# A gated cross-attention and feed-forward kernel: the first feed-forward layer by two levels of seven products, over blocks of 1024 tokens

## The chip, the cores and the metric

The kernel runs on one core of a Trainium2 chip. The core has five engines with a queue of instructions each: TensorE (PE in the profile, with its weight loads as PEld), VectorE (DVE), ScalarE (ACT), GpSimd (POOL) and SyncE (SP), which here issues nearly all DMAs. TensorE multiplies a stationary 128x128 tile (lhsT) by a moving tile and writes to PSUM, which has eight banks of 512 float32 per partition; the other engines work on SBUF, and ACT and DVE on PSUM too. The metric is the device time of one execution in microseconds (us), the median over runs. All data is float32.

## What is computed

Four sequences of 2048 tokens of width 512 attend to 128 context tokens each, and then pass a feed-forward network (FFN) with one of eight experts, chosen once per sequence. Cut to what matters:

```
x = x + tanh(g_xattn) * xattn(layernorm(x), ctx)
z = layernorm(x)                                   # (4, 2048, 512)
top1 = argmax(mean(z, tokens) @ Wr + br)           # one expert for each sequence
h = relu(z @ W1[top1] + b1[top1])                  # 512 -> 2048
out = x + tanh(g_ffn) * (h @ W2[top1] + b2[top1])  # 2048 -> 512
```

## The kernel before

**Stages.** For the first sequence ("batch" 0) attention and normalization of its four blocks of 512 tokens run ahead of everything else, with pools of their own (line 226 on). After that the FFN of batch b runs block by block, and the attention of batch b+1 is woven in: `attention` and `route` are generators, and the loop from line 671 advances them by one step at some of the `yield`s of `ffn`. Attention leaves x (after attention) and the normalized z, transposed, in DRAM tiles (`x1d`, `z2d`); `route` picks the expert, reads its number into a register (line 361) and loads its biases. The order in which instructions are emitted gives their priority; a scheduler places them on the engines' queues and adds the semaphores.

**The two FFN layers.** Each layer's matrix product is split into 2x2 quarters on each side and done with seven products of quarters in place of eight (the form with 15 sums). `chain` (line 447) issues the matmuls of one product into one bank. The sums of the operands are made beforehand: of z on DVE (`z_combine`, line 475), of the weights on POOL (`w1_combine`, `w2_combine`), of h on DVE (lines 557, 558, 617, 618). The seven results are put together by ACT copies (lines 529, 592) and DVE additions that read PSUM (lines 533 to 554, 607 to 642). Where two products belong to the same output, the second goes on accumulating in the bank of the first (`fresh` is False).

The first layer (lines 499 to 561) runs over a block of 512 tokens and four groups of hidden columns: each of the seven products of a group takes 2 x 2 matmuls with 256 moving columns, 112 matmuls for a block. W1 is loaded anew for each block and group (`w1_load`, 256 KB pieces in a pool of 13 buffers), and its sums are made anew on POOL. Line 522 applies bias and relu on ACT. The second layer (lines 589 to 647) has seven products of 16 matmuls each, 112 for a block; W2 is loaded once for each batch and its sums are made once. Line 584 adds each result, scaled, to the residual `xr`, which POOL has given the bias (line 564), and two stores per block write the output.

**PSUM.** After the first phase there are five banks for the FFN (`ps_f`), two for transposes and one for attention.

## Time and profile before

| | us |
|---|---|
| median of 3 runs | 1820.86 (1819.43 to 1821.22) |
| profiled execution | 1823.6 |
| its span, first to last instruction | 1821.8 |
| mean granted TensorE clock, share of full speed | 0.988 |

| stretch, us | PE busy | DVE busy | ACT busy | POOL busy | granted clock | GB/s |
|---|---|---|---|---|---|---|
| 0 to 50 | 37.10 | 26.64 | 5.45 | 4.68 | 0.97 | 282 |
| 50 to 100 | 46.50 | 28.30 | 29.37 | 4.22 | 0.93 | 171 |
| 100 to 150 | 37.77 | 15.54 | 7.01 | 28.18 | 0.86 | 273 |
| 150 to 200 | 36.93 | 22.94 | 14.84 | 25.63 | 0.83 | 106 |
| 300 to 600 | 300.00 | 134.49 | 62.59 | 103.13 | 1.00 | 116 |
| 1671.07 to 1767.90, one FFN block alone | 96.83 | 36.96 | 16.81 | 20.26 | 1.00 | 54 |

The span begins with the first instruction and ends with the last; the run's own time lies a little above it. A busy time counts an engine from the start of an instruction to its end; for PE matmuls are pipelined, so that a busy PE need not be at its peak. The granted clock is the share of TensorE's full clock that the throttle let through. In the groups of instructions a line has the source line, the engine, the operation, output and input by name, shapes and count, then the busy time, the mean of one in ns, and the engine's idle time just before with what ended it.

### The profile page before, as it was taken

How to read it: one execution, taken by the hardware profiler on the slowest of the kernel's cores; microseconds unless marked ns; L12 is line 12 of the kernel's file. 1: busy time of each engine (PE TensorE's matmuls, PEld its weight loads, DVE VectorE, ACT ScalarE, POOL GpSimd, SP SyncE). 2: the span in 40 equal slices, each digit the busy share in tenths (PEclk: the TensorE clock that was granted, in tenths of full speed). 3: DMA queues.
4: the chain of work that ended last, by engine and by line, in shares of the span. 5: the costliest groups of instructions: out<-in, count | busy, mean ns of one | idle time of the engine just before them, and what ended most of it. 6: DMA issues, size and time to landing. Idle time of an engine off the chain costs nothing.

```text
span 1821.8 us, 21727 instructions
## 1 busy us (share of the span) xinstructions
PE 1766.8 (97%) x8336; PEld 1515.9 (83%) x8336; DVE 829.1 (46%) x1283; ACT 393.1 (22%) x941; POOL 555.6 (30%) x376
## 2 busy tenths in 40 slices
PE   7977999999999999999999999999999999999998
PEld 5546788888888888788888888788888888888887
DVE  4615446454434645464353545555344434444342
ACT  1422213121111313223030322313021111212030
POOL 0137215032325504124051813204043632314030
PEclk9988999999999999999999999999999999999999
DMA  7373334241243425343132434314133322212100
GB/s 288 157 297 110 130 149 152 85 159 52 93 139 108 147 87 168 116 156 117 65 98 106 137 129 162 129 68 145 36 116 116 116 70 92 71 71 92 69 24 24
DMA packets 62167, 211.45 MB, mean 116 GB/s; under 512 B 8048, under 2 KB 8048, under 8 KB 47344
## 3 DMA queue, kind: packets, MB, share of 16 engines
q1 hardware_dynamic: 60336, 208.20, 32.7%
q10 hardware_dynamic: 1728, 1.86, 0.3%
q8 instruction: 66, 1.08, 0.2%
q14 instruction: 37, 0.30, 0.0%
HBM read 158.13 MB, written 51.90 MB: 115 GB/s over the span
## 4 chain that ended last, share of the span: by engine, by line
PE 89%; DVE 3%; POOL 3%; DMA 2%; issue 2%; ACT 1%; SPq 0%; ACTq 0%; POOLq 0%; DVEq 0%
PE Z L451 24%; PE V L451 23%; PE X L451 22%; PE Y L451 12%; PE psc L161 3%; PE pav L191 2%; PE pt L214 1%; PE pv L292 1%; DVE st L146 1%; DVE x L192 1%; DMA w<-in_W_dram 1%; POOL w2t L444 1%; DMA bqk_t<-in_bqk_dram 1%; PE pk L266 1%; POOL w2t L441 0%
## 5 line engine op out<-in xcount | busy, mean ns | idle before, releaser
L522 ACT ACTIVATE h<-c,b1T 128x256 f32<-128x256 f32 x384 | 174.0, 500 | 515.3 <-DVE c L541 267.3
L451 PE MATMUL X<-zt,w 128*128 128x256 f32 x1024 | 246.4, 383 | 0.8 <-ACT r L529 0.7
L451 PE MATMUL X<-w,h 128*128 128x256 f32 x1024 | 230.0, 381 | 2.7 <-ACT r L592 2.5
L451 PEld LDWEIGHTS X<-w,h 128*128 128x128 f32 x1024 | 192.6, 190 | 34.6 <-ACT r L592 6.9
L451 PEld LDWEIGHTS X<-zt,w 128*128 128x128 f32 x1024 | 195.3, 192 | 31.0 <-issue 2.9
L406 POOL TENSOR_TENSOR w1t<-w,w1t 128x512 f32<-128x512 f32 x64 | 89.6, 1400 | 370.7 <-issue 368.5
L153 POOL TENSOR_TENSOR rstd<-ve,mhalf 128x4 f32<-128x4 f32 x32 | 33.7, 1052 | 411.5 <-DVE ve L152 360.6
L403 POOL TENSOR_TENSOR w1t<-w,w 128x512 f32<-128x512 f32 x64 | 87.5, 1367 | 200.9 <-PE Z L451 200.4
L529 ACT COPY r<-X 128x512 f32<-128x512 f32 x64 | 36.3, 568 | 441.2 <-PE X L451 441.2
L451 PE MATMUL Y<-s,w1t 128*128 128x256 f32 x512 | 121.7, 380 | 4.3 <-POOL w1t L404 4.3
L451 PE MATMUL Z<-zt,w 128*128 128x256 f32 x512 | 123.2, 383 | 0.0
L451 PE MATMUL V<-s,w1t 128*128 128x256 f32 x512 | 121.5, 379 | 0.0
L451 PE MATMUL Z<-zt,w1t 128*128 128x256 f32 x512 | 121.1, 379 | 0.0
L451 PE MATMUL V<-s,w 128*128 128x256 f32 x512 | 120.9, 379 | 0.0
L557 DVE TENSOR_TENSOR hS<-h,h 128x512 f32<-128x512 f32 x64 | 97.0, 1516 | 49.8 <-ACT h L522 49.7
L451 PE MATMUL Z<-w,h 128*128 128x256 f32 x512 | 117.1, 379 | 0.0
L451 PE MATMUL Z<-w2t,h 128*128 128x256 f32 x512 | 115.8, 379 | 0.0
L451 PE MATMUL V<-w2t,hS 128*128 128x256 f32 x512 | 115.3, 379 | 0.0
L451 PE MATMUL Y<-w2t,hS 128*128 128x256 f32 x512 | 115.1, 379 | 0.0
L451 PE MATMUL V<-w,h 128*128 128x256 f32 x512 | 114.1, 379 | 0.0
L451 PEld LDWEIGHTS Y<-s,w1t 128*128 128x128 f32 x512 | 96.2, 190 | 17.6 <-POOL w1t L404 5.1
L451 PEld LDWEIGHTS Y<-w2t,hS 128*128 128x128 f32 x512 | 97.0, 190 | 16.4 <-issue 3.8
(112 smaller groups left out, 2519.7 us busy)
## 6 DMA issues: line engine op xcount, KB each, us to landing
w<-in_W_dram SPq DMA_DIRECT2D x256, 256.0 KB, 2.7
xT<-in_xT_dram SPq DMA_DIRECT2D x16, 1024.0 KB, 4.9
x<-in_x_dram SPq DMA_DIRECT2D x16, 1024.0 KB, 5.5
x1d<-x SPq DMA_DIRECT2D x16, 1024.0 KB, 3.9
xr<-x1d SPq DMA_DIRECT2D x16, 1024.0 KB, 5.1
z2d<-zT SPq DMA_DIRECT2D x16, 1024.0 KB, 4.5
zt<-z2d SPq DMA_DIRECT2D x16, 1024.0 KB, 4.8
w<-in_W_dram SPq DMA_DIRECT2D x16, 1024.0 KB, 4.9
```

The costliest lines, as they stand in the source:

```text
L146: nc.vector.bn_stats(st, xt[:, t, :])
L153: nc.gpsimd.tensor_tensor(rstd, ve, mhalf, ALU.pow)
L161: nc.tensor.matmul(psc[:, t, :], lhsT=xTt[:, kc, t * P : (t + 1) * P], rhs=Mb[:, kc, :], start=kc == 0, stop=kc == KC - 1,)
L191: nc.tensor.matmul(pav, lhsT=pT[:, t * P : (t + 1) * P], rhs=Vb, start=True, stop=True)
L192: nc.vector.scalar_tensor_tensor(xt[:, t, :], pav, coef[:, t : t + 1], xt[:, t, :], ALU.mult, ALU.add)
L214: nc.tensor.transpose(pt[:, t * P : (t + 1) * P], z[:, t, kc * P : (kc + 1) * P], ident)
L403: eng.tensor_tensor(t1, b12, b11, ALU.subtract)
L406: eng.tensor_tensor(t4, b21, t2, ALU.subtract)
L451: nc.tensor.matmul(bank[:, c, :], lhsT=left(k, c), rhs=right(k, c), start=fresh and c == 0 and k == 0, stop=c == cols - 1 and k == ks - 1, ...
L522: nc.scalar.activation(dst[:, 2 * g + c, :], src[:, c, :], AF.Relu, bias=b1T[:, f : f + 1])
L529: nc.scalar.copy(r1, X)
L557: nc.vector.tensor_tensor(hS[:, sl, :], h["21"][:, sl, :], h["22"][:, sl, :], ALU.add)
```

## The change

The first layer is done by two levels of seven products. The work is cut into stages: a block of 1024 tokens and one half of the hidden columns (`fh`). On the outer level z (1024 x 512) and W1 (512 x 1024) are each cut into quarters and combined to seven operands; each outer product is cut and combined again to seven inner products of 128 x 256 x 256, which take two matmuls each. The second layer keeps one level, on the half of the hidden columns that the stage has, for two halves of the output's token pairs (`cp`); the partial output of the first half of the columns goes to DRAM (`y1d`) and is loaded as the residual of the second.

What goes with it:

- `inner` gives the seven inner products with three banks X, Y and Q. The sums that were made by DVE are now continued in PSUM: ACT copies X to Y and later Y to Q, and further products accumulate on the copy. Six matmuls named "begin" write all six banks once before.
- `ffn1` interleaves the inner products of one outer product with the last three of the one before it. The results of two quadrants are summed by DVE (`done`), those of the other two by DVE and POOL (`summed`), and their activations are put off (`waiting`).
- The weight sums are made once per batch and half by `stage_w1` and `stage_w2` on POOL and stored to DRAM (`W1d`, `W2d`), the stores put off by some steps (`later`, `older`). For the first half of batch 0 `stage_w1_first` makes them on DVE and hands the first tiles on directly. The FFN loads all weights through a ring of eight tiles (`fetch`), 14 for each layer and stage.
- `z_prepare` loads z for 1024 tokens and makes both levels of sums on DVE, during the second layer of the stage before.
- Attention normalizes x in place after its store, which is cut in two; the transposed z shares the pool of x's transpose. `ps_t` has one bank instead of two, `ps_f` six instead of five.
- The weaving is by a clock: each step of the FFN adds 0.87 or 3.46, attention advances one step per 2.2, staging one per 1.45.
- `layouts` arranges W1 and W2 for these loads.

The core of the diff; the two layers' old code (lines 375 to 445 and 465 to 647) is removed:

```diff
     for t in range(4):
...
+            if t % 2:
+                nc.sync.dma_start(x1d[b, blk][:, t - 1 : t + 1, :], xt[:, t - 1 : t + 1, :])
             yield
-        nc.sync.dma_start(x1d[b, blk], xt)
...
-        z = zp.tile([P, 4, H], F32, tag="z", name=f"z_{b}_{blk}")
+        z = xt
...
+    def inner_sums(eng, b, fh, pc, src, lo, n, slot, kinds="AB"):
+        new = stp.tile([P, 3, 4, P], F32, tag="new", name="new", bufs=2)
+        b11, b21, b22, b12 = (src[:, lo : lo + n, i, :] for i in range(4))
+        t3, t2, t4, t1 = (new[:, 0:n, i, :] for i in range(4))
+        for o, l, r in ((t1, b12, b11), (t2, b22, t1), (t4, b21, t2), (t3, b22, b12)):
+            eng.tensor_tensor(o, l, r, ALU.subtract)
+            yield
...
+    def stage_w1(b, fh, eng):
+        for pc in range(2):
+            flush()
+            base = stp.tile([P, 4, 4, P], F32, tag="base", name="base")
+            tt = stp.tile([P, 3, 4, P], F32, tag="tt", name="tt")
+            w1_base(b, fh, pc, base)
+            yield from settle(4)
+            for _ in outer_sums(eng, base, tt):
+                yield from settle(1)
+            for src, lo, n, slot in ((base, 0, 3, 0), (base, 3, 1, 3), (tt, 0, 3, 4)):
+                for _ in inner_sums(eng, b, fh, pc, src, lo, n, slot):
+                    yield from settle(1)
+            yield from settle(AGE + 1)
...
+    def fetch(freed=0):
+        ring["freed"] += freed
+        while ring["issued"] < min(ring["freed"] + NW, len(items)):
+            st, kind, i = items[ring["issued"]]
...
+    def inner(product, copied, summed, done):
+        t = {}
+        def m1():
+            t["X"] = bank("X")
+            product(t["X"], 1, True)
+            t["Y"] = bank("Y")
+            nc.scalar.copy(t["Y"], t["X"])
+        def m7():
+            t["Q"] = bank("Q")
+            product(t["Q"], 7, True)
+            t["s7"] = copied(t["Q"])
+        def m6():
+            product(t["Y"], 6, False)
+            nc.scalar.copy(t["Q"], t["Y"])
+        def m2():
+            product(t["X"], 2, False)
+            done(11, t["X"])
+        def m5():
+            product(t["Y"], 5, False)
+            summed(22, t["s7"], t["Y"])
+        def m4():
+            product(t["Q"], 4, False)
+            summed(21, t["s7"], t["Q"])
+        def m3():
+            product(t["Y"], 3, False)
+            done(12, t["Y"])
...
+        level1(5, 7, 4, ALU.add)
+        yield
+        level1(6, 5, 1, ALU.subtract)
+        level2(5)
+        yield
...
+            def summed(j, a, v):
+                c = first(j) if m == 1 else ctile()
+                nc.vector.tensor_tensor(c, a, v, ALU.add)
+                if m != 1:
+                    sums(m, j, c, nc.gpsimd, c)
+            def done(j, v):
+                if m == 1:
+                    nc.scalar.copy(first(j), v)
+                else:
+                    sums(m, j, v, nc.vector)
...
+        for i in range(8):
+            cur = group(i) if i < 7 else None
+            for k, (who, m) in enumerate((
+                (cur, 1), (last, 5), (cur, 7), (last, 4), (cur, 6), (last, 3), (cur, 2)
+            )):
+                if who:
+                    due = len(waiting) if k in (0, 3) else 0
+                    who[m]()
+                    for _ in range(due):
+                        relu(*waiting.pop(0))
+                    yield
...
+            fetch((cur is not None) + (last is not None))
+            last = cur
...
+            cur[2]()
+            for k in (slice(0, 2), slice(2, 4)):
+                nc.vector.tensor_tensor(
+                    h[12][:, k, cs], h[12][:, k, cs], hS[:, k, cs], ALU.subtract
+                )
+                nc.vector.tensor_tensor(hS[:, k, cs], hS[:, k, cs], h[11][:, k, cs], ALU.add)
+            yield
+            cur[4]()
+            if cp == 0:
+                s2(1)
+            yield
+            cur[5]()
+            store(cp, 1)
+            yield
+            cur[3]()
+            store(cp, 0)
+            yield
...
+    for _ in range(6):
+        bk = bank("begin")
+        nc.tensor.matmul(
+            bk.rearrange("p a q -> p (a q)"), lhsT=ident, rhs=cq, start=True, stop=True
+        )
...
+    run(z_prepare(0, 0))
+    run(route(0))
+    stage_w1_first(nc.vector)
+    bias2_load(0)
+    staged_upto[0] += 1
+    fetch()
+    run(stage_w2(0, 0, nc.gpsimd))
...
+        for blk in range(NF):
+            for fh in range(2):
+                for _ in ffn1(b, blk, fh):
+                    tick(0.87)
...
+                for _ in ffn2(b, blk, fh):
+                    next(prep, None)
+                    tick(3.46)
```

## The prediction

> **What bounds the kernel now.** I read the page's busy shares first, then the chain of work that ended last, then PE's waits, then the groups for durations.
>
> ```profile
> PE 1766.8 (97%) x8336; PEld 1515.9 (83%) x8336; DVE 829.1 (46%) x1283; ACT 393.1 (22%) x941; POOL 555.6 (30%) x376
> ```
>
> TensorE is busy 97% of the span; no other engine reaches half. A busy PE alone proves little, so the chain, in order of time (start, duration, work), around the end of one FFN block:
>
> ```profile
> 1373.54 1.73 PE Z L451 x8
> 1375.26 1.73 PE V L451 x8
> 1376.99 6.91 PE X L451 x32
> 1383.90 0.86 PE Z L451 x4
> 1384.76 7.04 PE X L451 x32
> 1391.80 6.04 PE Z L451 x28
> ```
>
> The chain is matmul after matmul. A float32 matmul shows as two instructions, so a first-layer product (4 matmuls) is 1.73 us and a second-layer one (16) is 6.91 us. The same product returns at 1574.24, 1671.07 and 1767.90: 96.83 us per 512-token block without attention work, 224 matmuls, **0.4323 us each**. After the first 200 us PE waited for 7.6 us in all:
>
> ```profile
> PE Y L451 <- POOL w1t L404: 3.3, 1, 3.3
> PE X L451 <- ACT r L592: 2.5, 2, 1.3
> PE pav L191 <- DVE x L192: 1.8, 2, 0.9
> ```
>
> So time follows the count of matmuls, until something else gets in PE's way. The start is different: the first FFN matmul is at 121.78 us, and over the next 42 us PE is busy 29.84 us at a granted clock of 0.83 (the columns are PE, PEld, DVE, ACT, POOL busy, clock, DMA share, GB/s).
>
> ```profile
> 122.00:132.00 10.00, 8.34 (x29) 6.21 (x30) 0.69 (x1) 0.58 (x1) 9.92 (x6) 0.82 1.04 416
> 122.00:164.00 42.00, 29.84 (x124) 24.93 (x125) 14.56 (x25) 8.06 (x18) 41.76 (x31) 0.83 0.54 206
> ```
>
> The rows from which the rest is priced:
>
> ```profile
> L522 ACT ACTIVATE h<-c,b1T 128x256 f32<-128x256 f32 x384 | 174.0, 500 | 515.3 <-DVE c L541 267.3 <-DVE c L554 151.7 <-DVE c L549 96.0
> L406 POOL TENSOR_TENSOR w1t<-w,w1t 128x512 f32<-128x512 f32 x64 | 89.6, 1400 | 370.7 <-issue 368.5
> L557 DVE TENSOR_TENSOR hS<-h,h 128x512 f32<-128x512 f32 x64 | 97.0, 1516 | 49.8 <-ACT h L522 49.7
> L537 DVE TENSOR_TENSOR u<-u,Z 128x512 f32<-128x512 f32 x64 | 44.0, 688 | 48.3 <-PE Z L451 47.0
> L584 DVE SCALAR_TENSOR_TENSOR xr<-c,gf,xr 128x512 f32<-128x512 f32 x48 | 36.8, 766 | 1.5
> L482 DVE TENSOR_TENSOR zt<-zt 128x512 f32<-128x512 f32 x16 | 11.0, 685 | 0.0
> L617 DVE TENSOR_TENSOR hS<-hS,h 128x1024 f32<-128x1024 f32 x32 | 40.5, 1267 | 53.9 <-PE V L451 53.9
> L529 ACT COPY r<-X 128x512 f32<-128x512 f32 x64 | 36.3, 568 | 441.2 <-PE X L451 441.2
> ```
>
> **Removed: matmuls.** First layer: 49 products of 2 matmuls per stage (1024 tokens, half the hidden columns), 98, against 112 for the same work before. Second layer: 2 x 7 products of 2 x 4 = 112, unchanged. All keep 256 moving columns and the 0.4323 us. A stage is 210 x 0.4323 = 90.8 us (42.4 + 48.4), 16 stages 1452.5 us, against 3584 x 0.4323 = 1549.4 us: **-96.8 us**.
>
> **Added on VectorE.** Per stage: 28 adds with one PSUM operand (0.688) 19.3; 4 + 12 sums of hidden tiles at 0.685 alone, 1.516 beside POOL, 11-24; 12 additions to the output (0.766) 9.2; on alternate stages the bias, 4 x 1.22 = 4.9, or the sums of z, 4 x 1.22 + 28 of 256 elements. No row has 256; between 0.167 (128x8) and 0.685 a line gives 0.42, so 16.6; mean 10.8. Attention of the next batch 13.4 (the rows of lines 146 to 199 over 16 blocks). Together 64 to 77 of 90.8 us, against about 39 of 96.8 before. Worst are the second layers that carry the z sums: 9.2 + 8.2 to 18.2 + 16.6 + 7.1 = 41 to 51 of 48.4 us, six times over three batches. VectorE stays under PE, but runs of several us come before what PE waits for.
>
> The spread stands on line 557: shortest 0.678, median 1.544, and its neighbours without POOL at work 0.685. So about 0.83 us is lost per meeting. The Trainium skill ("SBUF — State Buffer", section "SBUF: two separate sides") goes further against this change: a VectorE operation with two SBUF inputs and a GpSimd operation that reads SBUF exclude each other for a whole instruction, the loser "fully blocks". By that rule each of some 30 such operations per stage could wait a whole 1.40 us instead of 0.83, 17 us more VectorE per stage, and the sum below would move to rival C.
>
> **Added on ScalarE.** Per outer product three copies (X to Y, the seventh product out of PSUM, Y to Q), 1.70 us; 32 activations per stage at 0.45 to 0.50. First layer 12 + 1 + 15 = 28 of 42.4 us, second 3.4, attention 9.0 (lines 175 to 217): 41 of 90.8.
>
> **Added on POOL.** 14 sums x 1.40 = 20 per stage; weight sums 84 per batch (60 of 512 elements' worth). About 47%.
>
> **Added on DMA.** In MiB: weight ring 207 (28 loads of 384 or 512 KB per stage), staging 97, residuals 64, z 16, attention 64, constants 8: 456 MiB, 478 MB against 211.45. At the 416 GB/s of the row above that is 1150 us, under 70% of the span; all goes through SP's queue, some 60 issues of 0.35 us per stage. The exception is the first stage: ring 10, residuals 4, the first W1 and W2 staging 12, the second half's 10, attention 9.5 MiB, 48 MB in 91 us = 530 GB/s, 24 us late, of which the ring of eight tiles (three outer products, about 15 us) covers most.
>
> **What lands on PE's path.** (a) Turns, where a product must continue in a bank that ACT or DVE has just read. In the chain X ends at 1383.90 and resumes at 1384.76: 0.86 us for a 0.58 us copy, so 0.28 of signalling, with two matmuls of Z pulled into the gap. In the first layer two outer products are interleaved: three other products, 2.6 us, lie between a copy and its use, so nothing shows; without that cover each turn costs 0.86. In the second layer product 3 follows 5 in the same bank: 0.766 + 0.28 = 1.05 us, twice a stage. If the next product's matmuls fill it as Z did, about 0.4 stays. With 0.4 for the last outer product, which has no partner, **1.2 us per stage, 15 stages, +18**; bounds 0 and 5 us (1.05 plus one 1.22 us operation ahead of it on VectorE, twice, and 0.4): 0 to +75. Behind a late VectorE, its additions and then product 3 and the ring's releases queue; POOL's sums delay only activations two thirds of an outer product later.
>
> New waits on memory, each costed at 0 with its cover: z overwrites x in place, so ACT waits there for the stores of x1d (2.6 us per 512 KB on the page's DMA list) with the copies of the FFN queued behind it; two paced steps of 2.2 us lie between. The residuals of the second token half are loaded into the buffers of the first, store plus load about 2.6 + 3, first needed 7 us later by VectorE, behind which the hidden sums queue. On SP such a waiting store holds the weight loads behind it; the ring's 15 us cover it. Without these covers each costs PE 2 to 5 us, which is rival C again.
>
> (b) The start. The route is at 114 us as now; then two loads of 1 MiB (some 7 us at 416 GB/s with 2 us of latency, against 256 KB pieces before) and the first sums, so 124 instead of 121.8: **+2** (-5 to +8; the first attention pass gets more buffers, but z now waits for the store of x1d that it overwrites). In the first stage VectorE also makes the weight sums, 56 of 128 elements (0.29 on the same line) and 8 of 512, 22 us, so 41 to 47 + 6 of attention against 42.4 of matmuls, and the DMA is late by up to 9 beyond its cover: **+13** (0 to +30). The old start loses some 12 us over 122 to 164 too, which stays in the base. Six extra matmuls of 512 columns (about 0.86 each, twice the 256-column price) lie in the idle gap before the first weights: 0; without that gap 5.2. The end keeps one addition and one store: 0 (-1 to +2).
>
> **Sum.** 1821.8 - 96.8 + 18 + 2 + 13 = 1758.0 us of span. The profiled execution was 1823.6 with this span, so +1.8, and the median of the runs is 2.7 below that: **1757 us**.
>
> The Trainium skill ("PSUM — Partial Sum Buffer", section "The four PSUM rules") holds that only zero is a safe ScalarE seed for an accumulation and that others go through the PE. No run here shows what a bank does with such a seed. Seeding by a 512-column identity product instead would, by the estimate above, put two more 0.86 us products in each of 112 + 32 sets, 248 us, and undo the change; the code copies instead.
>
> **Rivals.**
> - A, the forecast: 1740 to 1775. Chance 0.50.
> - B, nothing new shows: turns filled, start covered: 1821.8 - 96.8 + 2, less 0.9, about 1726 (1715 to 1740). For it: PE's 7.6 us of waits now. Against: VectorE at 70 to 85% and no spare bank. 0.20.
> - C, a crowded VectorE: meetings with POOL on top, 4 us per stage, in the second layer: 60 instead of 18, 1799 (1780 to 1812). For it: line 557. Against: PSUM-operand adds show 0.688 whatever POOL does. 0.18.
> - D, slower: ACT's copies are late in the first layer. In the last outer products ACT has 1.7 + 3.6 + 1.4 of attention = 6.7 us per 6.05 us of matmuls, in order, and an activation that waits for POOL holds the copy behind it. One exposed turn per outer product, 112 x 0.86 = 96: 1757 + 96 = 1853. It decides from 64 us, 0.57 us per outer product. Against: the 2.6 us of cover. 0.09.
> - E: DMA delivers too little. Slower only below 478 MB in some 1.7 ms, 281 GB/s, against 416 when pressed; 240 GB/s would give about 2 ms. 0.03.
>
> **How the numbers follow.** The point is A's. The range holds A, most of B and C's lower half: 1722 to 1805; A's own range is 1740 to 1775. What this kernel's measurement can tell from no change is about 0.2%, 3.6 us. Faster: A, B and nearly all of C, 0.87; within it C's top, 0.02; slower D and E, 0.11.
>
> **What would show it.** 3360 FFN matmuls, with products of the second layer still 3.46 us per 8; gaps of under 1 us before product 3 of the second layer, released by VectorE's L584-like additions; no PE wait on ScalarE in the first layer (D if there are 112 of them); VectorE near 65% and DMA near 70%; the first FFN matmul near 124 us. I am wrong if PE waits total more than 60 us after 220 us, or if ring loads are what releases matmuls.

## The result, and the profile after

The change made the kernel slower: 1914.41 us (median of 4 runs, 1909.92 to 1921.93) against 1821.04 us (1819.43 to 1824.66) of the kernel before on the same chip, a ratio of 1.0514 (95% interval 1.0475 to 1.0553). 1757 was predicted, 1805 was the top of the range. The profiled execution took 1909.92 us with a span of 1908.1.

The page's busy line of the changed kernel:

```profile
PE 1739.5 (91%) x7900; PEld 1446.0 (76%) x7900; DVE 1039.8 (54%) x1807; ACT 607.4 (32%) x1339; POOL 639.1 (33%) x552
```

The count of TensorE instructions fell by 436: twice the 224 matmuls that were taken away, less twice the six that were added. Only 27.3 us of busy time went with them, though, and the span grew. No engine but TensorE passes 54%; the answer can't be an engine that is full on average. TensorE's waits of the changed kernel from 200 us on (what waited, for whom; us in all, times, longest):

```profile
PE Y L607 <- ACT Q L635: 36.7, 18, 5.8
PE Y L607 <- DVE hS L903: 17.1, 13, 3.6
PE psc L195 <- DVE sc L199: 16.7, 9, 4.7
PE Y L607 <- DVE c L781: 12.8, 14, 1.9
PE Y L607 <- DVE xr L872: 11.4, 7, 3.1
PE Y L607 <- ACT Y L626: 7.0, 3, 3.5
```

Where there were 7.6 us of waits there are now 117 (with five smaller kinds), the largest on ScalarE's copies in the first layer. From 220 us on they sum to 110.7; the prediction had named more than 60 as its sign of being wrong. In the last sequence, which has neither attention nor weight sums beside it, the chain of the changed kernel (start, duration, work) is as before:

```profile
1624.70 0.86 PE Q L607 x4
1625.56 0.86 PE Y L607 x4
1626.43 1.73 PE X L607 x8
1628.15 0.86 PE Y L607 x4
```

Matmul after matmul, at the old price, so the loss lies in particular stages. To find it I added up, from the trace's instruction times, how much longer each interval from one TensorE instruction to the next is than the undisturbed one (0.216 us for 256 columns), and call that the *loss*; it holds waits and slowed matmuls alike. From the first FFN matmul on, the kernel before loses 39.1 us and the changed one 219.1. The sum closes: 1821.8 - 96.8 (matmuls) + 4.1 (first FFN matmul at 125.9 instead of 121.8) - 39.1 + 219.1 = 1909.1, against 1908.1 measured. A loss can shift by 1 to 2 us with the value taken as undisturbed for attention's short matmuls. By the 16 stages, and by first (L1) and second layer (L2):

```
                          what lies beside it            L1 lost   L2 lost
stage 0                   staging and attention             32.6      17.2
stages 2,3,6,7,10,11      staging of the next sequence      60.8      40.3
stages 1,5,9              attention's end, staging's start  37.9      11.9
stages 4,8                attention                          4.0       4.3
stages 12-15              nothing                            4.3       5.8
```

Stages 12 and 14, with nothing beside them, take 93.0 and 92.7 us; the prediction had 90.8 + 1.2. What a loss looks like: the timeline of POOL, those of VectorE and ScalarE (start, duration, operation; in brackets the idle time before and what ended it), then four-microsecond stretches of TensorE alone (PE busy, clock, DMA share, GB/s), all of the changed kernel in stage 10.

```profile
1344.23 1.28 POOL L420 TENSOR_TENSOR tt<-base,tt 128x512 f32<-128x512 f32 x1
1345.46 1.01 POOL L429 TENSOR_TENSOR new<-base,new 128x384 f32<-128x384 f32 x1
1346.41 1.01 POOL L429 TENSOR_TENSOR new<-base 128x384 f32<-128x384 f32 x1
1347.37 1.27 POOL L742 TENSOR_TENSOR u<-r,c 128x512 f32<-128x512 f32 x1
...
1350.38 0.99 POOL L429 TENSOR_TENSOR new<-base,new 128x128 f32<-128x128 f32 x2
1351.32 2.48 POOL L745 TENSOR_TENSOR c<-u,c 128x512 f32<-128x512 f32 x2
```

```profile
1343.86 0.69 DVE L781 TENSOR_TENSOR c<-s,Y 128x512 f32<-128x512 f32 x1 [0.97 <-ACT h L712]
1345.56 0.69 DVE L781 TENSOR_TENSOR c<-s,Q 128x512 f32<-128x512 f32 x1 [1.01 <-PE Q L607]
```

```profile
1344.63 0.59 ACT L772 COPY s<-Q 128x512 f32<-128x512 f32 x1 [0.31 <-PE Q L607]
1352.62 0.91 ACT L712 ACTIVATE h<-c,b1T 128x256 f32<-128x256 f32 x2 [7.41 <-POOL c L745]
1353.43 0.58 ACT L635 COPY Q<-Y 128x512 f32<-128x512 f32 x1
```

```profile
1344.00:1348.00 4.00, 4.00 (x20) 1.00 0.08 27
1348.00:1352.00 4.00, 0.91 (x5) 1.00 0.88 238
1352.00:1356.00 4.00, 1.94 (x5) 0.76 1.05 345
1356.00:1360.00 4.00, 4.00 (x17) 0.81 0.89 261
```

POOL is never idle here, but most of what it does is weight sums (L420, L429); the first layer's sum u (L742) and then c (L745) stand in its queue between them. VectorE had made the operands of the two sums of L745 by 1344.55 and 1346.25; the first of them starts at 1351.32. ScalarE sits for 7.41 us in front of the activation that waits for that c, with the copy Y to Q behind it, and TensorE, which needs the copied bank, loses 5.3 us there. The clock falls as well: the stretches after the gap show 0.76 and 0.81 in the mean, and the trace's clock record has 0.50 from 1354.07 to 1357.48.

The start of the changed kernel, with the columns of the prediction, to be set against the line of 122 to 164 us before:

```profile
126.00:168.00 42.00, 32.83 (x136) 24.84 (x135) 37.34 (x103) 16.30 (x42) 11.11 (x9) 0.91 0.70 229
```

VectorE's 37.34 of 42 us are weight sums, adds and attention, where the prediction had 41 to 47 plus 6 for the first layer of this stage.

### The profile page after: what moved, and what is told of

The parts are those of the page before. It is cut to its first block, busy times and chain, and to the rows that moved or that the text cites. A ratio compares the mean times of both kernels' runs of the same rounds, so it can differ in the third digit from the quotient of the medians.

```text
span 1908.1 us, 22980 instructions
## 1 busy us (share of the span) xinstructions
PE 1739.5 (91%) x7900; PEld 1446.0 (76%) x7900; DVE 1039.8 (54%) x1807; ACT 607.4 (32%) x1339; POOL 639.1 (33%) x552
## 2 busy tenths in 40 slices
DMA packets 186659, 479.86 MB, mean 251 GB/s; under 512 B 17328, under 2 KB 71088, under 8 KB 175920
## 5 line engine op out<-in xcount | busy, mean ns | idle before, releaser
L607 PE MATMUL Y<-z,w 128*128 128x256 f32 x1344 | 352.3, 395 | 61.7 <-ACT Q L635 38.3
L607 PEld LDWEIGHTS Y<-z,w 128*128 128x128 f32 x1344 | 258.3, 197 | 119.5 <-ACT Q L635 47.4
L607 PE MATMUL Y<-w,hS 128*128 128x256 f32 x1024 | 243.8, 389 | 18.0 <-DVE hS L903 17.1
L607 PEld LDWEIGHTS Y<-w,hS 128*128 128x128 f32 x1024 | 196.5, 195 | 56.1 <-DVE hS L903 25.0
L607 PE MATMUL Q<-w,h 128*128 128x256 f32 x1024 | 233.8, 380 | 0.0
L607 PE MATMUL Q<-z,w 128*128 128x256 f32 x896 | 225.3, 389 | 3.0 <-DVE c L733 1.7
L607 PE MATMUL X<-z,w 128*128 128x256 f32 x896 | 222.2, 385 | 0.7 <-PE X L607 0.7
L626 ACT COPY Y<-X 128x512 f32<-128x512 f32 x144 | 82.5, 573 | 424.5 <-PE X L607 420.6
L607 PEld LDWEIGHTS Q<-w,h 128*128 128x128 f32 x1024 | 193.4, 191 | 27.7 <-issue 2.4
L607 PEld LDWEIGHTS Q<-z,w 128*128 128x128 f32 x896 | 174.0, 197 | 30.5 <-DVE c L733 2.5
L607 PEld LDWEIGHTS X<-z,w 128*128 128x128 f32 x896 | 171.4, 194 | 27.0 <-issue 3.3
L420 POOL TENSOR_TENSOR tt<-base 128x512 f32<-128x512 f32 x30 | 38.5, 1285 | 296.5 <-DMA base<-in_W_dram 268.8
L635 ACT COPY Q<-Y 128x512 f32<-128x512 f32 x144 | 82.4, 572 | 159.0 <-PE Y L607 156.7
```

Source lines behind the costliest of these rows:

```text
L420: eng.tensor_tensor(o, l, r, ALU.subtract)
L607: nc.tensor.matmul(bank[:, c, :], lhsT=left(k, c), rhs=right(k, c), start=fresh and c == 0 and k == 0, stop=c == 1 and k == ks - 1, skip_g ...
L626: nc.scalar.copy(t["Y"], t["X"])
L635: nc.scalar.copy(t["Q"], t["Y"])
```

## The experiments

The table gives the losses of each kernel in the groups of stages above. Where an interval stands, the time is the median of 4 to 10 executions; without one it is a single execution. Executions of one kernel spread over 12 us (the changed kernel) and 23 us (e11), so a difference of that size between single executions says little. The losses are those of the profiled execution: for e11 (1866.95), e13 (1907.37) and e15 (1818.36) the slowest of its kernel, for the changed kernel (1909.92) and e14 (1829.53) the fastest. The kernel before, timed beside each, took 1818.99 to 1826.85 us.

```
                              us   ratio (95%)              st.0   staging   1,5,9    all
                                                          L1  L2   L1   L2   L1  L2
changed kernel             1914.4  1.0514 (1.0475-1.0553) 33  17   61   40   38  12   219
e1_sums_dve                1845.2                         28  25    7   40   18  18   152
e2_staging_no_sums         1815.7                         22  13    8   14   36  12   124
e3_staging_no_dma          1971.0                         33  18  121   37   40  12   279
e4_stores_off_sync         1876.3                         31  21   25   55   21  14   183
e5_residuals_two           1885.1                         46   4   55   36   25  10   191
e6_zt_own_buffer           1884.2                         47   8   37   50   21   9   183
e7_staging_paced           1901.8                         33  13   47   34   38  15   210
e8_hidden_sums_first       1834.1                         27  24   16   29   17   8   140
e9_woven_work_in_place     1937.0                         43  14   37   67   33  12   245
e10_both                   1885.6                         36  13   24   45   30  15   192
e11_sums_first_z_batched   1856.8  1.0168 (1.0122-1.0213) 27  26   20   41   24  17   175
e12_late_attention         1822.1  1.0003 (0.9986-1.0019) 32   2   23    7   21  18   130
e13_late_att.._pool_sums   1899.8  1.0427 (1.0410-1.0445) 34   4   55   30   27  19   214
e14_later_attention        1835.3  1.0080 (1.0064-1.0097) 32   4   12   20   22  17   140
e15_two_paces              1812.3  0.9950 (0.9929-0.9972) 32   2   11   20   18  17   127
e16_tokens_first           1838.9  1.0086 (1.0068-1.0105) 16  16   16   37   17  19   145
e17_quarter_sums           1838.1                         26  16   17   19   35  11   145
```

**Sums off POOL.** `e1_sums_dve`:

```
             if m != 1:
-                sums(m, j, c, nc.gpsimd, c)
+                sums(m, j, c, nc.vector, c)
```

> The 14 sums per first layer that POOL made move to VectorE; POOL keeps the weight staging and the powers. Times against 1910 us of the changed kernel. Theory P (POOL's queue is in order: the sums of the FFN stand behind staging work that waits for a DMA, the activations wait for them, and the copies for PE stand behind the activations): the loss of PE in the first layers of the seven stages that have staging and no cover (3, 5 to 7, 9 to 11; 84 us) falls to some 2 us each; 1825 to 1855 us. Theory D (the loads are late because the DMAs carry 480 MB): no more than 10 us either way, 1900 to 1920. Theory V (VectorE is too full): 14 x 0.69 = 9.6 us more per stage on VectorE makes it worse, 1930 to 1970.

1845.22 us, 69 us less, with VectorE at 62% instead of 54. The first layers of the staging stages lose 7 us instead of 61, those of 1, 5 and 9 half, and the wait on ScalarE's copy, 38.3 us over the whole changed kernel, is all but gone:

```profile
PE Y L607 <- ACT Q L635: 5.0, 5, 1.6
```

So the first layer's loss comes by way of the sums on POOL, and more work on VectorE costs less than that.

**What on POOL delays them.** `e2_staging_no_sums` keeps the staging's loads and stores without POOL's weight sums; `e3_staging_no_dma` keeps the sums without the loads and stores, for the last three sequences.

```
-            eng.tensor_tensor(o, l, r, ALU.subtract)          # e2, on POOL
...
-            w1_base(b, fh, pc, base)                           # e3
+            if b == 0:
+                w1_base(b, fh, pc, base)
```

> The weight staging keeps all its DMAs, but the sums on POOL are left out for all but the very first half batch: what is stored are unsummed tiles of the base, so the FFN's weights are not the right ones. Theory P: POOL has the FFN's sums alone and nothing in its queue waits for a DMA; the first layers with staging lose some 2 us each, and the powers of the attention come in time; 1800 to 1840 us. Theory D: the traffic is as before, 1895 to 1920. Theory V: fewer meetings of POOL and VectorE, 10 to 25 us less, 1885 to 1900.

> For batches 1 to 3 the weight staging keeps its sums on POOL, made from one base tile that is loaded once, but its loads and stores are left out, and the FFN loads the staged weights of batch 0: wrong weights, the ring's traffic unchanged, about 73 MiB less in all. Theory P: POOL still works as much, but never waits for a DMA with the FFN's sums behind it; the first layers of stages 5 to 7 and 9 to 11 lose 2 to 4 us each instead of 10 to 16, batch 0 stays; 1840 to 1870 us. If POOL's work itself were too much, without any waiting: no change, 1895 to 1915. Theory D: 1820 to 1850, and the second layers of stages 6, 7, 10, 11 (33 us lost) gain as much as the first. Theory V: no change.

e2: 1815.72 us, 94 us below the profiled execution of the changed kernel; the first layers of the staging stages lose 8 us, the second 14. The traffic by itself costs little there. Stages 1, 5 and 9 are untouched: 36 us in the first layer, against 38. e3: 1970.97 us, and TensorE's longest wait in its list (290 to 1400 us) is 51 us:

```profile
PE Y L620 <- ACT Q L648: 97.2, 9, 51.4
```

It missed its question, and taught another thing. With no load to wait for, the scheduler that orders the queues put the staging sums of all three batches forward into one stretch: the trace shows POOL on staging sums back to back from 395 to 475 us, with no first-layer sum between them, and for 15 to 20 of every 20 us until 655. Stages 2 and 3 lose 148 us, and stages 6, 7, 10 and 11, which had no weight sums left beside them, some 10 us in all. So e3 says nothing of staging without transfers in those stages; it says that weight sums ahead in POOL's queue are enough to stop TensorE without any transfer.

Two accounts remained. POOL may stand still for a staging load with the first layer's sums behind it; its list of waits shows 269 us in 22 waits on `base`. Or the weight sums ahead in the queue are just long. `e7_staging_paced` tried the first by more paced steps between load and sum:

```
-    AGE = 3
+    AGE = 5
...
-            yield from settle(4)
+            yield from settle(12)
...
-                    clock[1] += 1.45
+                    clock[1] += 1.0
```

> The changed kernel with the first layer's sums on POOL as they are; only the paced order of the staging is changed: twelve steps instead of four between the load of a weight tile and its first sum, five instead of three between a sum and its store, and a step each 1.0 us instead of 1.45. POOL's work and every transfer are the same. Theory P (POOL stands in its in-order queue waiting for a staging load, 12 us at a time, and with it the first layer's sums behind): POOL's wait for the staging loads, 269 us, falls below 80; the first layers of stages 2, 3, 6, 7, 10 and 11 lose under 4 us each instead of 5 to 15, and the time falls from 1910 by 50 to 70, to about 1850. Rival V (meetings of POOL and VectorE in SBUF, or simply POOL's amount of work): the first layers lose what they lost and the time stays above 1895.

A miss: 1901.78 us, first layers 47, and POOL still waits 250 us for staging loads, so the edit did not remove what it aimed at. That these waits are mostly harmless shows in the changed kernel's trace. For each first-layer sum on POOL I took the time from the end of VectorE's operation that makes its operand to its own start, and what POOL did meanwhile:

```
changed kernel   delay us   POOL on weight sums   on other first-layer sums   idle   longest
stage 2              34.7                  18.5                        16.6    0.5       7.0
stage 6              27.3                  18.9                         8.8    0.6       6.9
stage 10             53.0                  38.3                        15.1    0.6       7.2
stage 12             10.2                   0.0                         8.5    1.8       3.8
```

(sums over the stage's 14 operations). POOL is next to never idle while one of them could run. `e17_quarter_sums` tests the second account: the loads, the stores and the number of weight sums on POOL are the same, and each sum works on a quarter of the columns (0.25 to 0.64 us on average, by form, instead of 0.5 to 1.3).

```
+                q = P // 4
-            eng.tensor_tensor(o, l, r, ALU.subtract)
+                eng.tensor_tensor(o[:, :, 0:q], l[:, :, 0:q], r[:, :, 0:q], ALU.subtract)
```

> The changed kernel, its first-layer sums on POOL, every load, store and wait of the staging as it is, and the same number of staging sums on POOL, each on the first quarter of its columns alone: the other three quarters of the staged sums are left as they were, so the weights read by the products are not the ones wanted. Theory P (POOL stands waiting in its queue for a staging load or store, the first layer's sums behind it): waits are the same, so the first layers of stages 2, 3, 6, 7, 10 and 11 lose 45 us and more of their 61, and the time stays above 1880. Theory O (POOL is hardly ever idle while a first-layer sum is ready, by the trace 0.6 to 1.9 us a stage; what holds the sum back is staging sums placed ahead of it in the queue, 12 to 38 us a stage): with sums of 0.4 to 0.5 us instead of 1.0 to 1.3 these first layers lose under 20 us in sum and the time falls to about 1850 (1910 less 40 of the first layers and some 20 of what meets VectorE).

1838.11 us; first layers 17 instead of 61, second layers 19 instead of 40. POOL's wait for the loads and TensorE's wait for the copy in e17:

```profile
POOL tt L440 <- DMA base<-in_W_dram: 318.6, 25, 28.9
PE Y L631 <- ACT Q L659: 14.6, 15, 2.4
```

The waits for loads are longer than in the changed kernel (318.6 against 268.8 over the whole run) and most of the loss in the staging stages has gone. It is the length of the weight sums in the queue. Shorter sums also hold VectorE up less, but in these first layers that is little: 17 to 19 us of VectorE's work in each are additions with an operand in PSUM, which took 0.65 to 0.69 us with or without POOL at work, and its other sums were held up by 2 to 3 us a layer in the changed kernel. Nor is the queue too full on average: over a whole first layer with staging POOL is 71 to 83% busy (44% in stage 12). But the weight sums stand in it back to back, in runs of 4 to 16 that last 4 to 19 us with at most three first-layer sums among them, and a first-layer sum that becomes ready during a run waits for the end of a good part of it. The paced steps of 1.45 us do not keep the weight sums apart.

**The queues' order.** `e9_woven_work_in_place` binds what attention and staging give to the engines behind the instruction emitted last, so that the scheduler can't bring it forward:

```
+                    with behind(ALL):
+                        more = next(staged, StopIteration)
```

> The changed kernel, its sums on POOL, with one thing added: what attention and staging give to VectorE, ScalarE and POOL at each paced step is bound behind the instruction that was emitted last on that engine, so that the scheduler that orders the queues can't bring it forward into the work of the outer products before. No instruction and no transfer is added or left out. Theory H (the queues' order is made from estimated times in which loads land early; the sums and statistics brought forward stand at the head of an in-order queue before their data has landed, and the outer products' work behind them): the losses of the first layer in the stages with staging (2, 3, 6, 7, 10, 11) fall from 49 us in sum to under 20, those of stages 1, 5 and 9 from 38 to under 20, and the time falls from 1910 by 50 or more, to below 1860. Rival: the order as emitted is no better, since four steps of 1.45 us are less than the 7.5 us that a staging load takes; then these sums stay within a quarter of 49 and 38 and the time above 1890.

1937.01 us, worse. The first layers of the staging stages do fall, from 61 to 37, as they should if weight sums brought forward stand in the way; the second layers rise from 40 to 67, and stage 0 by 7. Binding everything to the emitted order costs more than it saves; that the weight sums brought forward are the harmful part of the reordering is read from these columns and was not tested alone.

**What is left in the second layer.** All the following have the sums on VectorE, as e1. `e4_stores_off_sync` issues the staged stores from POOL's queue, `e5_residuals_two` gives the residual tiles two buffers and the ring six tiles instead of eight, `e6_zt_own_buffer` gives the transposed normalized tokens a buffer, also with a ring of six.

```
-            nc.sync.dma_start(dst, src)                                   # e4
+            nc.gpsimd.dma_start(dst, src)
-    NW = 8                                                                # e5, e6
+    NW = 6
-                xr[cp, i] = xrp.tile(..., tag=f"xr{i}", name="xr", bufs=1)   # e5
+                xr[cp, i] = xrp.tile(..., tag=f"xr{i}", name="xr", bufs=2)
-        zT = xTp.tile([P, KC, TB], F32, tag="xT", ...)                    # e6
+        zT = xTp.tile([P, KC, TB], F32, tag="zT", ...)
```

> The first layer's sums are on VectorE, as in e1_sums_dve, and the stores of the staged weight sums are issued from POOL's queue, behind the sums that they store, instead of from SyncE's, where they stood waiting for POOL (some 135 us of waiting in three groups of the queue's waits) with the loads of the ring and of the residuals behind them. Theory Q (what is left in the second layer of the staging stages, 1.7 to 11 us a stage and 45 us in stages 2, 3, 6, 7, 10 and 11 together, is SyncE's queue held up by stores that wait for POOL): the second layers of these six stages lose under 3 us each, the waits of TensorE on hS fall from 23 to under 8 us, and the time falls from 1845 by about 30 to about 1815. Rival R (the residual buffers alone: the load of the second half waits for the store of the first, whatever stands on the queue): the second layers lose what they lost, and the time stays within 1838 to 1850. Rival S: issuing on POOL costs it or VectorE so much that the first layers lose again, over 1850.

> The first layer's sums are on VectorE, as in e1_sums_dve; the residual tiles have two buffers each instead of one, and the weight ring six tiles instead of eight to make room. Theory R (VectorE waits for residuals whose load waits for the store of the tile's last use, 37 us on y1d and 47 on out in the queue's waits; behind it stand the sums of hidden tiles that TensorE waits for): the second layers of all stages 1 to 11 lose under 3 us each where e1_sums_dve lost up to 11, the waits on hS fall from 23 to under 8 us, and the time falls from 1845 to about 1815. Theory Q (SyncE's queue behind stores that wait for POOL): the second layers lose what they lost, within 15 us in sum, and the time stays at 1838 to 1850. A ring of six instead of eight may cost by itself: then matmuls wait for the loads of w, which no kernel here has shown yet.

> The first layer's sums are on VectorE, as in e1_sums_dve; the transposed normalised tokens get a buffer of their own instead of the one that the next block's transposed tokens use, with the weight ring at six tiles to make room (in the start-up pass four and four buffers instead of five shared ones). Theory X (in the stages with attention the load of the next block's transposed tokens waits for the store of the last one, 45 us in the queue's waits, and TensorE's score products wait for that load, 12 us and more): stages 1, 5 and 9 lose under 5 us in the first layer instead of 2 to 8, SyncE's wait for that store is gone, and the time falls from 1845 to about 1830. Rival: the loss there is ScalarE's and POOL's order around the statistics and the normalising in place; then stages 5 and 9 lose 7 us and more as before and the time stays within 1838 to 1850.

All three are slower than e1, by 31 to 40 us. The theories of SyncE's stores (Q) and of the shared buffer (X) find no support; each edit brings a cost of its own, so they are not ruled out either. e5 and e6 did remove what they aimed at (the waits on hS fell from 23.2 to 8.1 us, SyncE's wait for the store of z2d from 45.5 to 3.8) and lost it elsewhere. VectorE of e5 in stage 10:

```profile
1316.47 0.69 DVE L745 TENSOR_TENSOR c<-u,X 128x512 f32<-128x512 f32 x1 [0.24 <-PE X L607]
1328.01 1.82 DVE L835 TENSOR_TENSOR xr<-xr,b2g 128x1024 f32<-128x1024 f32 x1 [10.85 <-DMA xr<-x1d]
```

L835 is the second layer's bias on a residual tile, here placed into the first layer's work. VectorE stands at it from 1317.2 us, its load is issued only at 1321.0, and TensorE waits 9.8 us for the adds behind it. The loss with a ring of six has no run that separates it from this, but the traces show a part of it: TensorE waits 24.3 us for weight loads in e5 and 15.3 in e6, against 0.7 in e1.

`e8_hidden_sums_first` orders VectorE instead: hidden sums first, residual additions bound behind them. Its second product reads h[12] after the subtraction that belongs behind it. `e10_both` adds e9's binding.

```
+            with behind():
+                bias(cp, 1)
+                cur["add"](21, held[0])
+                cur["add"](22, held.pop())
+                bias(cp, 0)
+                cur[2]()
```

> The first layer's sums are on VectorE, as in e1_sums_dve; in the second layer the sums of hidden tiles that products 3 and 5 need are given to VectorE ahead of every addition to the residual tiles of the same token half, and those additions are bound behind them in its queue. Nothing else moves. Theory R (in the second layer VectorE stands waiting for a residual load, with the hidden sums that TensorE needs queued behind; with two residual buffers the waits on hS fell from 23 to 8 us): the waits on hS fall below 8 us, the second layers of stages 1 to 11 lose under 4 us each (66 us in sum in e1_sums_dve, under 40 here), and the time falls from 1845 to about 1818. Rival M (VectorE is late because its operations meet POOL's and because the sums of z come in long runs): the waits on hS stay above 15 us and the time within 1838 to 1850. If a late residual load now holds the banks, the wait moves to products that follow the additions (xr), and less than 10 us is won.

> The edits of e8_hidden_sums_first and e9_woven_work_in_place together, with the first layer's sums on VectorE. If the losses are separate, they add: the second layers under 40 us, the first layers of stages 1 to 11 (32 us in e1_sums_dve) under 20, and the time about 1800, under the 1821 of the kernel before. If binding the woven work costs VectorE more waits than it saves, the time is above that of e8_hidden_sums_first.

1834.08 us for e8: no wait on hS is left, and the second layers of stages 2, 6 and 10 lose 1.7 us in sum (15.4 in e1). Those of 3, 7 and 11 still lose 27. VectorE in stage 11:

```profile
1425.94 4.15 DVE L691 TENSOR_TENSOR z<-z 128x256 f32<-128x256 f32 x5
1430.02 0.74 DVE L886 SCALAR_TENSOR_TENSOR xr<-Q,gf,xr 128x512 f32<-128x512 f32 x1
1430.68 3.09 DVE L691 TENSOR_TENSOR z<-z 128x256 f32<-128x256 f32 x9
```

and POOL at that time:

```profile
1423.41 3.46 POOL L429 TENSOR_TENSOR new<-tt 128x384 f32<-128x384 f32 x2 [13.68 <-DMA W1d_310B<-new]
1426.83 2.31 POOL L429 TENSOR_TENSOR new<-tt,new 128x384 f32<-128x384 f32 x2
```

Of the first five sums of z three meet POOL and take 1.21 us each; the other two and the nine take 0.41 (one starts every 0.34). The addition that TensorE waits for 2.5 us is behind them. e10, 1885.58, shows again that the emitted order is slower here.

**Towards a better version.** `e11_sums_first_z_batched` keeps the second product's operand as it should be and makes 8 sums of z out of 28. `e12_late_attention` also moves the woven attention of stage 0 back; `e14_later_attention` further. `e13_late_attention_pool_sums` is e12 with the sums back on POOL. `e15_two_paces` takes e12's paces for the first sequence and e14's for the rest; `e16_tokens_first` also loads tokens before transposed tokens.

```
-        clock = [0.0, 0.0, 0.0]
+        clock = [0.0, 0.0, 45.0 if b == 0 else 0.0]      # e14: 70.0
-                clock[2] += 2.2
+                clock[2] += 1.9 if b else 2.0            # e12: 2.0, e14: 1.9
-                clock[1] += 1.45
+                clock[1] += 1.25 if b else 1.35          # e12: 1.35, e14: 1.25
```

> The first layer's sums on VectorE; in the second layer the hidden sums ahead of every residual addition that needs them not (here the second product still reads its own operand: its sum comes behind it); and the sums of z, in e8_hidden_sums_first 28 small operations of 256 elements per block that took 0.83 us each when POOL worked and 0.36 otherwise, are made as 8 of 1024 and 768 elements. Theory M2 (the loss that is left in the second layers of stages 3, 7 and 11, 27 us in e8_hidden_sums_first, is VectorE's run of small operations that each meet an operation of POOL): these three second layers lose under 4 us each, and the time is about 1815 (1834 less 16 to 20). Rival R2 (it is the residual load of the second token half after all): they lose what they lost, and the time stays above 1828.

> e11_sums_first_z_batched with the woven attention of the second sequence starting 45 us later in the first stage, where the staging of the other half of the hidden columns runs too, and both paced a little faster (2.0 us a step instead of 2.2, 1.35 instead of 1.45). Theory S0 (the first stage loses its 50 us because attention's loads, the staging and the ring ask for more than the DMA delivers there, and because attention's rstd waits on POOL behind staging sums): the first stage loses 30 us or less, stage 1 no more than 8, and the time is 15 to 20 below that of e11_sums_first_z_batched, about 1798. Rival: attention's own chain (scores, exp, transpositions, each waited for by TensorE) costs the same wherever it stands; then the loss moves to stage 1 and the time is within 6 us of that of e11_sums_first_z_batched.

> e12_late_attention with one line undone: the first layer's sums are on POOL again, as in the changed kernel. Theory P (the first layer's sums on POOL queue behind staging sums that wait for a load or a store, and ScalarE's copies behind the activations that wait for them): it costs here what it cost there, 60 to 70 us, so the time is 1875 to 1895, and TensorE's waits on ScalarE's copy of Q come back, 30 us and more. If the reordering in the second layer, the batched sums of z and the later attention were what the changed kernel lacked, the time stays below 1840.

> e12_late_attention with the woven attention of the second sequence starting 70 us after the first stage's begin instead of 45, and both paced faster (1.9 us a step instead of 2.0, 1.25 instead of 1.35). Theory S0 (attention and staging meet in the first stage; in e12_late_attention the first two stages still lose 34 and 20 us): the two lose under 45 in sum and the time is 5 to 12 us below 1822. Rival: what is left in the first layer of the first stage is its own ring loads, issued behind the staging loads on SyncE's queue, and VectorE's weight sums; then the first stage still loses 30 us or more, the attention's part only moves on to stage 1, and the time is within 5 us of 1822.

> e12_late_attention with its pace kept for the first sequence and the faster pace of e14_later_attention (1.9 and 1.25 us a step) for the later ones. By the stages of the two profiles, e12's stages 0 to 5 (704 us, against 720) and e14's stages 6 to 11 (608, against 612) and the same end would add up to about 1815; within 4 us of 1822 if the order of the queues in one stage depends on the pace in the others.

> e15_two_paces with the woven attention loading the tokens, which its statistics on VectorE read first, one step before the transposed tokens, which TensorE reads later and whose buffer is still being stored. Theory X2 (VectorE's statistics wait for a load that stands on SyncE's queue behind one that waits for a store, and first-layer sums behind them): stages 4, 5, 8 and 9 lose 10 us less in sum and the time is 1805 to 1812. Rival: TensorE's scores then wait longer for the later load, and the time is that of e15_two_paces or above.

e11 missed: stages 3, 7 and 11 lose 39 us in the second layer, more than in e8, and its runs spread over 23 us. Over the run VectorE waits 65 us for the loads of z where it waited 11 in e8; I did not follow it further. e12 is level with the kernel before, 35 us below e11: stage 0 loses 34 us instead of 52, but most of the gain is in the second layers of the staging stages (41 to 7), which was not expected of it; the waits for z are 28 us there. e13 costs 78 us over e12 (1899.84 against 1822.06): POOL's sums are the price in this order too. e14 came out 13 us above e12, which neither account foresaw. Its stage 0 loses as much as e12's, 36 against 34, so there the rival holds; stage 2, into which attention now reaches further, and stage 4 lose 12 us more in sum. e15 is the best, **1812.32 us, 0.5% below the kernel before** (0.9929 to 0.9972). Its page's busy line:

```profile
PE 1709.3 (94%) x7900; PEld 1428.1 (79%) x7900; DVE 1142.3 (63%) x1871; ACT 613.0 (34%) x1339; POOL 367.9 (20%) x328
```

In the profiled execution it still loses 127 us. e16 (1838.85) won 16 us in the first layer of stage 0 and lost more than that in the second layers of stages 0 and 3.

## Why the prediction was wrong

- **Matmuls, -96.8: right.** The instruction count and the stages with nothing beside them say so.
- **Steady stages, +18 (1.2 us each): within its bounds only where nothing lies beside.** Stages 12 to 15 lose 10.1 us, 2.5 each, twice the term; with the sums on VectorE (e1) 0.9. Stages 1 to 11 lose 159.2 against some 13 in the sum, and the kernel before loses 15.0 there. This term carries nearly all of the error, and it lay beyond its own upper bound of +75 because that bound priced a late VectorE only.
- **The step that failed** is the clause "POOL's sums delay only activations two thirds of an outer product later". It took POOL's time at its mean, about 47% busy, and put the delay at nothing for TensorE. The sizes were not at fault (33% busy over the span, 80 weight sums a sequence for its 84, 1.38 us a first-layer sum for its 1.40); the runs of weight sums in the queue were not in it. Behind them first-layer sums start up to 7 and 8 us late, and an activation that waits holds the copy behind it. That is the mechanism of rival D, right in kind and misplaced: D put one exposed turn of 0.86 us on all 112 outer products, and the six stages with staging show 12 waits on the copy to Q, of 2.7 us on average and up to 5.8. By e17 the length of the weight sums is worth 44 us in those first layers; by e1 taking the sums off POOL is worth 54 there and 20 more in stages 1, 5 and 9.
- **Rival C, a crowded VectorE, holds beside it**, in the second layer as it said: stages 1 to 11 lose 56 us there (40 + 12 + 4). Shorter weight sums (e17) win back 21 of the 40 in the staging stages, and no weight sums (e2) 26. Its ground, the meetings with POOL, is in the trace: 98 of VectorE's sums with two operands in SBUF were held up until an instruction of POOL had ended, by 0.68 us on average against the 0.83 of the prediction. So each does wait out the other engine's instruction, but the 17 us a stage that the prediction worked out for that case did not come: the delays sum to 67 us in 16 stages. Ordering the residual additions took away the wait on hS (e8). "Without these covers each costs PE 2 to 5 us" named the residual loads; the cover of 7 us did not hold: VectorE's list shows 80 us in 19 waits for x1d, up to 12.2 us, and 37 in 9 for y1d. I gave A, C and D as alternatives; they came together, in different stages.
- **First stage, +13 (0 to +30): mis-sized, within its bounds.** It loses 49.8 where the kernel before loses 24.1 until 290 us: +26. e12, with the late attention, loses 34 there and e11, without it, 52. The first layer's part stays at 32 in e12, e14 and e15; by the list of single losses it falls on ring loads issued behind staging loads, VectorE's weight sums and attention's scores. I tried no run on each of these alone; e16, which has attention's tokens loaded ahead of the transposed ones, has 16 there and 16 instead of 2 in the second layer.
- **Start, +2: measured 4.1.** **DMA:** 479.86 MB against 478, and 73% of the engines' time in the main queue where "under 70%" stood. No run makes the amount of traffic the bound: e2 has all of it and takes 1815.7 us.
- **Not in the working at all: the clock after a gap.** In the changed kernel, from 120 us on, 14 gaps of 3.2 us or more (61.5 us in sum) are followed within 8 us by 26.7 us of slowed matmuls, 1.9 us each. The trace's clock record reads 0.50 in 18 stretches of 3.4, 6.8 or 10.2 us after the first FFN matmul, 102 us in sum, and 1.00 otherwise; matmuls in them lost some 37 us. So about a sixth of the 219 us is not waiting but matmuls at half the clock, which the prediction's prices of waits left out. The Trainium skill ("TensorE: Matmul & The Clock Gate", section "HAM oscillation — how this bites in real kernels") warns of idle gaps above about 3.4 us, after which TensorE starts again at the lower clock. These rows agree for long gaps: half clock followed 13 of the 14. The limit is not sharp here: a gap of 2.4 us was followed by 2.5 us of slowed matmuls, and one of 3.2 by 0.1.

Open: the first layers of stages 1, 5 and 9. The weight sums are not the cause there (36 us without them in e2 and 35 with short ones in e17, against 38); moving the first layer's sums to VectorE wins 20, and 18 remain (21 in e6, with a buffer for the transposed tokens). Open too are the ring of six by itself, and how much of each result is the scheduler's new order rather than the edit. e5 and e6 each removed the wait that they aimed at and were slower.

## What to carry to other kernels

An in-order engine's share of the span, or of a stage, does not say how late its work is when two streams meet on it: look for how long one stream holds the queue at a time (here 4 to 19 us), and follow what stands behind the first instruction that is late. Saving matmuls on a kernel that TensorE bounds pays only if what replaces them (copies, sums, staging) stays out of the queues on which the next product waits; here 97 us of matmuls were paid for with 180 us of waits and slowed matmuls. A stall of TensorE above some 3 us should be priced with the slow matmuls behind it, here about 2 us.

## What the runs showed of the hardware

- In the changed kernel TensorE's granted clock was 1.00 or 0.50, the latter in stretches of 3.4 to 10.2 us. It followed 13 of 14 gaps of 3.2 us or more, with 1.9 us of slowed matmuls behind each on average, and some gaps from 2.4 us on.
- A VectorE sum with two operands in SBUF and a sum on POOL held each other up for the rest of the one that came first. In the changed kernel each of the 98 delayed VectorE sums ended a fixed time after the end of a POOL instruction: 0.28 us with 256 columns, 0.55 with 512, 1.08 with 1024 (alone they take 0.41, 0.69 and 1.22). Delayed sums on POOL ended 0.86 us (384 columns, 1.0 alone) or 1.13 us (512, 1.27 alone) after the end of a VectorE sum. The first layer's additions on VectorE with an operand in PSUM took 0.65 to 0.69 us whatever POOL did.
- Matmuls went on accumulating in banks that ScalarE had filled with sums other than zero (L626 and L635, 144 copies each in an execution), in banks that a matmul had written before, and the sums came out right.
- A wait that a profile lists for an engine can be only its lack of work: POOL's 269 us of waits for staging loads cost the changed kernel nothing that could be seen, and 319 us of them in e17 went with 72 us less of time (1838.11 against 1909.92 of the profiled run).
